# Scores and value products 512 queries wide, and eight context chunks transposed on VectorE

## The chip, the cores and the metric

The kernel runs on one core of one Trainium2 chip. The metric is the device time of one execution in microseconds; the time of a kernel is the median of its runs. TensorE is called PE below, its weight loads PEld, VectorE DVE, ScalarE ACT, GpSimd POOL, SyncE SP.

## The reference

One block of a network: cross attention of 4096 queries on 3202 context rows (8 heads of 64), a residual, then a small state-space scan of 64 states, and a row that is added to everything. All is fp32. Cut to what matters here:

```python
x = _layernorm(builder_state, g1, beta1)             # 4096 x 512 queries
base_n = _layernorm(base_state, g1, beta1)           # 3202 x 512 context rows
q, k, v = heads(q_in, Wq, bq), heads(kv_in, Wk, bk), heads(kv_in, Wv, bv)
scores = einsum('bhqd,bhkd->bhqk', q, k) * (1 / sqrt(HD))
attn = softmax(scores, axis=-1)
out = einsum('bhqk,bhkd->bhqd', attn, v)
x = residual + out.reshape(...) @ W_o.T + b_o
U = (_layernorm(x, g2, beta2) @ W_in.T + b_in) @ Bmat
s = silu(s @ A.T) + u_t                              # 4096 steps, 64 states
x = residual + states @ Cmat + mod
```

## The kernel before

**First stage, the context (to about 217 us).** The 3202 context rows are cut into 26 chunks of 128 keys (`NCH`), the last with 2 (`REST`). For each chunk c: `load_chunk` on SP, `norm_chunk` (statistics on DVE, factors on POOL, scaling on ACT), `turn_chunk` (four 128x128 transposes on PE into PSUM and one copy to `ct`, by DVE for odd chunks and by ACT for even ones), then four matmuls with `wv` for the values `pv`. After every fourth chunk (a group, `GC`) the keys `pk` of the group are made for four pairs of heads, 512 keys wide. Keys and values are stored to DRAM (`kd`, `vd`) as tiles of two chunks. Pieces of other work (weights, first queries) stand between, taken from the generator `side`.

**Second stage, attention.** The queries are cut into 8 blocks of 512 (`QB`, index Q), each block into two halves of 256 (`QU`). A unit is one half of one block for one pair of heads hp (two heads a = 0, 1 fill 128 rows); there are 64 units. A unit has 13 steps (`NDC`); a step takes two chunks of keys b = 0, 1 (the last step one chunk). A step is four pieces:
- `scores` (L713, PE): for each chunk four matmuls of 64 rows x 64 columns x 256 queries, one for each quarter of the PE array. They fill the PSUM tile `s` of 128 x 1024. A matmul in fp32 stands in the trace as two records, so eight records make one chunk.
- `weights` (L790, ACT): the exponential of `s` into an SBUF tile `p`, with the shift of the pair of heads.
- `product` (L847, PE): for each chunk four matmuls of 64x64x256 with the value tile, summed over the whole unit in the PSUM tile `po`. It has two banks, one for each half k of the keys, of which the first 256 columns are used. There is one `po` (ring `o`, one buffer).
- `add` (L798, DVE): sums `p` into `acc`, from which the denominators come.

At the second step `rest` (L784, DVE) adds the weights of the two last keys. At a unit's end: `product` first adds the last two keys (L835); `output` (ACT, L892) copies the first bank of `po`, `join` (DVE, L896) adds the second, and after that `po` is free for the next unit's first product. `fold` (DVE, L805) adds the two chunks' halves of `acc`; `swap` (ACT, L817) and `gather` (DVE, L822) add the halves of the partitions, `sums` (PE, L875) the keys, `denominators` (ACT, L914), `inverse` (DVE, L919), `scale` (DVE, L930). In the same stage the next block's queries are normalized, transposed on DVE in 32x32 squares (`flip`, L1049) and put in place by 16 small DMAs for each half block (`move`, L1061), projected (`heads`, L332), and the finished half blocks are projected (`project`: `outs` L1108, `inputs` L1165) and stored.

`load_k` and `load_v` (L379, L387) bring the tiles from DRAM on SP, 10 and 6 steps ahead; the units of the second half of a block use the tiles of the first again, apart from the last block, whose units run half by half.

**Third stage.** The scan over the states and the output rows, from about 1830 us on; it overlaps the last units.

**What sets the order.** In the second and third stage each piece is given to a planner (`Plan`): its engine, an estimated cost in ns, the pieces it comes after, a due time, and the buffers that it takes and gives back (rings, as `s`=2, `p`=18, `o`=1). `order` runs a list scheduler over these numbers and fixes the order on every engine before the program is built: an engine that comes free takes the piece with the earliest due time among those that could start. The due times are a multiple of `STEP` = 2150, and the table `SHIFT` moves the due time of each sort of piece by a number of steps. On the chip each engine then works off its list in order, and waits on semaphores.

Of the kernel before, what the change touches and what calls it, by code (L numbers as in the profile page):

```python
# [20 lines left out]
P = 128  # L21
# [12 lines left out]
FIRST = 3  # L34
WARM = 17
# [34 lines left out]
class Plan:  # L70
# [15 lines left out]
        "row.store": 11.5, "fold": 2, "rows.outs": 0.75, "heads": -12, "sample": -3, "spread": 4.75,  # L86
        "query.flip": -11, "states": -5.5, "inverse": 4.75, "extra": 10, "scale": -57.75, "rest": -1,
        "row.mod": -17, "joined0": -14.25, "b": -15, "add.l": -23, "l.stats": -34.75, "last": -4.5,
        "base": -34.75, "inverse.l": -27, "rows.inputs": 3.5, "maximum": -13.5, "fall": -19, "query.stats": -8,
        "den": 4.5, "row.scaled": 12, "l.h": -7, "row.stats": -9.25,  # L90
# [100 lines left out]
def xattn_ssm_kernel(  # L191
# [178 lines left out]
    kp = actx.enter_context(tc.tile_pool(name="kp", bufs=NDC))  # L370
    kts, vts = {}, {}

    def load_k(i, c):

        Q, hp, half = units[i]
        if half == 0 or Q == NQB - 1:
            t = kp.tile([P, 2 * CK], F32, tag="k", name=f"k_{Q}_{hp}_{half}_{c}")
            n = blocks(c) * CK
            nc.sync.dma_start(t[:, :n], kd[hp, c, :, :n])  # L379
            kts[Q, hp, c] = t  # L380

    def load_v(i, c):
        Q, hp, half = units[i]
        if half == 0 or Q == NQB - 1:
# [9 lines left out]
    steps = [(i, c) for i in range(len(units)) for c in range(NDC)]  # L394
# [150 lines left out]
    cxs, xhs, cts = {}, {}, {}  # L545
# [37 lines left out]

    with tc.manual_schedule():
# [14 lines left out]
        for c in range(4, 5):  # L599
            load_chunk(c)  # L600
# [15 lines left out]
        for c in range(NCH):  # L616
            load_chunk(c + 5)
# [4 lines left out]
            norm_chunk(c + 3)  # L622
# [17 lines left out]
            turn_chunk(c + 2)  # L640
# [19 lines left out]
            for hp in range(NC):  # L660
                pk = kps.tile([P, 512], F32, tag="k", name=f"pk_{g}_{hp}")
                for i in range(NC):
                    nc.tensor.matmul(  # L663
                        pk[:, :n_g],
                        wk[:, i, hp * P : (hp + 1) * P],
                        ct[:, i, :n_g],
                        start=(i == 0),
                        stop=(i == NC - 1),
                    )
                ks = cin.tile([P, GC * CK], F32, tag="ks", name=f"ks_{g}_{hp}")  # L670
                nc.scalar.activation(  # L671
                    ks[:, :n_g], pk[:, :n_g], AF.Identity, bias=bias[:, NC + hp : NC + hp + 1]
                )
# [31 lines left out]
    def scores(w, c):  # L705
# [3 lines left out]
        for b in range(blocks(c)):  # L709
# [69 lines left out]
    def rest(w):  # L779

        t = extras[w["at"][:2]][:, :, w["at"][2], :]
        for k in range(2):
            r, to = slice(k * HD, k * HD + REST), w["acc"][:, :, 0, k * P : (k + 1) * P]
            nc.vector.tensor_tensor(to[r], t[r], to[r], ALU.add)  # L784

    def weights(w, c):

        nb = blocks(c)
        t = w["s"][c] = sp_.tile([CK, 2, 2, QU], F32, tag="s", name=f"p_{w['name']}_{c}")
        nc.scalar.activation(t[:, :, :nb, :], w["ps"][c][:, :, :nb, :], AF.Exp, bias=w["shift"])  # L790

    def add(w, c):

        nb, t = blocks(c), w["s"][c]
# [14 lines left out]
    def halves(w, k):  # L809
        return slice(k * HD, (k + 1) * HD), w["acc"][:, :, 0, k * P : (k + 1) * P]  # L810
# [13 lines left out]
    def product(w, c):  # L824
# [6 lines left out]
        if c == NDC - 1:  # L831
            for a in range(2):
                for k in range(2):
                    r = slice(k * HD, (k + 1) * HD)
                    nc.tensor.matmul(  # L835
                        w["po"][a * HD : (a + 1) * HD, k, k * P : (k + 1) * P],
                        vx[r, hp * P + a * HD : hp * P + (a + 1) * HD],
                        extras[Q, hp][r, a, half, :],
                        start=False,
                        stop=False,  # L840
                        skip_group_check=True,
                    )
        for b in range(blocks(c)):
            for a in range(2):
                for k in range(2):
                    r = slice(k * HD, (k + 1) * HD)
                    nc.tensor.matmul(  # L847
                        w["po"][a * HD : (a + 1) * HD, k, :QU],
                        vts[Q, hp, c][r, b, a * HD : (a + 1) * HD],
                        t[r, a, b, :],  # L850
                        start=(c == 0 and b == 0),
                        stop=(c == NDC - 1),
# [3 lines left out]
    def sums(w):  # L856
# [15 lines left out]
        for a in range(2):  # L872
            for k, (k0, k1) in enumerate(((0, HD), (HD, P))):
# [4 lines left out]
                    w["acc"][k0:k1, a, 0, of],  # L878
# [9 lines left out]

    def output(w):
        Q, hp, half = w["at"]  # L890
        o = o_t[Q, hp, half] = op.tile([P, QU], F32, tag="o", name=f"o_{w['name']}", bufs=12)
        nc.scalar.copy(rows_of(w, o), rows_of(w, w["po"][:, 0, :QU], True))  # L892

    def join(w):
        o = rows_of(w, o_t[w["at"]])
        nc.vector.tensor_tensor(o, rows_of(w, w["po"][:, 1, :QU], True), o, ALU.add)  # L896

    def finish(w, i, d, plan):
# [29 lines left out]
        def scale(part):  # L928
            o = o_t[w["at"]][:, part]
            nc.vector.tensor_tensor(o, o, w["rd"][:, part], ALU.mult)  # L930

        plan.add(("output", i), "ACT", 360, partial(output, w), [("product", i, NDC - 1)], d, ["o_"])
        plan.add(("join", i), "DVE", 430, partial(join, w), [("output", i)], d + 500, [],
                 [("o", ("product", i, 0))])
        acc = [("acc", ("add", i, 1))]
        if last:
            plan.add(("sums", i), "PE", 880, partial(sums, w), [("add", i, NDC - 1)], d + 1000, ["s"], acc)
            opened = ("inverse", i, 0)
        else:
            plan.add(("fold", i), "DVE", 680, partial(fold, w), [("add", i, NDC - 1)], d + 500)  # L940
            plan.add(("swap", i), "ACT", 760, partial(swap, w), [("fold", i)], d + 600, ["rd"])
# [22 lines left out]
    def from_(d):  # L964

        return ("scores", *divmod(min(int(d / STEP), len(steps) - 1), NDC))
# [77 lines left out]

    def flip(pair, xh, t):

        nc.vector.transpose(  # L1049
            pair.rearrange("p t h -> p (t h)").rearrange("p (g t r) -> p t g r", t=2, r=TB)[:, t],  # L1050
            xh.rearrange("p (g r) -> p g r", r=TB),
        )

    def move(xn, pair, a):

        n = 2 * TB
        of = pair[a * TB : (a + 1) * TB].rearrange("p t h -> p (t h)").rearrange(
            "p (c b k) -> p b c k", b=P // TB, k=n
        )
        for b in range(P // TB):  # L1060
            nc.sync.dma_start(xn[b * TB : (b + 1) * TB, :, a * n : (a + 1) * n], of[:, b])  # L1061
# [518 lines left out]
    def unit(plan, i):  # L1580
# [3 lines left out]
        s0 = i * NDC  # L1584

        def scores_(c):
# [4 lines left out]
            w["q"] = qt[Q, hp][:, half * QU : (half + 1) * QU]  # L1591
# [20 lines left out]
        for c in range(NDC):  # L1612
            d = (s0 + c) * STEP
            g = s0 + c - NDC + AHEAD
            old = [("product", *divmod(g, NDC))] if g >= 0 else []
            part = blocks(c) / 2
            plan.add(("scores", i, c), "PE", 864 * part, partial(scores_, c), q + old, d, ["s"],
                     [("q", ("heads", Q, hp))], "quarters")
            plan.add(("weights", i, c), "ACT", 200 + 861 * part, partial(weights, w, c),
                     [("scores", i, c), ("base", first)], d + 1000, ["p"],  # L1620
                     [("s", ("scores", i, c))])
            d += LAG * STEP
            p = ("p", ("weights", i, c))
            more, gives = [], [p]
            if c == NDC - 1:
                more, gives = [("extra", first)], [p, ("extra", ("extra", first))]
            plan.add(("product", i, c), "PE", 864 if part == 1 else 650, partial(product_, c),
                     [("weights", i, c)] + ([("product", i, c - 1)] if c else []) + more,
                     d + 1000, [] if c else ["o"], gives, "quarters")
            if c:  # L1630
                before = {1: ("weights", i, 0), 2: ("rest", i)}.get(c, ("add", i, c - 1))
                plan.add(("add", i, c), "DVE", 120 + 1120 * part, partial(add, w, c),
                         [("weights", i, c), before], d + 1200,
                         ["acc"] if c == 1 else [],
                         [p] + ([("p", ("weights", i, 0))] if c == 1 else []))
            if c == 1:
                plan.add(("rest", i), "DVE", 860, partial(rest, w), [("add", i, 1), ("extra", first)],
                         d + 1300, [], [("extra", ("extra", first))])
        d += 2000
        finish(w, i, d - 40 * STEP if w["last"] else d, plan)  # L1640
# [241 lines left out]
    with tc.manual_schedule():  # L1882
# [5 lines left out]
                xn=1, xh=2, max=2, rd=2, o_=12,  # L1888
# [5 lines left out]
        for i, (Q, hp, half) in enumerate(units):  # L1894
            d = unit(plan, i)
            if (hp, half) == (1, 0) and Q + 1 < NQB:
                queries(plan, Q + 1, i * NDC * STEP)
# [97 lines left out]
```

## Time and profile before

| what | value |
|---|---|
| median of 3 runs | 1946.28 us (1945.93 to 1947.35) |
| the profiled execution's own time | 1949.57 us |
| its span, first to last instruction | 1947.8 us |
| granted TensorE clock | 0.997 |
| busy PE, PEld, DVE, ACT, POOL | 1927.4, 1259.5, 1465.8, 1169.8, 216.5 us |

A busy time is the time in which at least one instruction of a group was in flight. PE matmuls overlap: a record lasts longer than the time until the next one starts, and four quarters of the array work at once. So a PE time is read here from the starts of records, not from their lengths. The timeline view has one row for a run of equal instructions: its start, its length, and the number of records. The view by stretches gives the busy time of each engine in a stretch. The view of groups gives line, engine, operation, tiles, shapes, and then busy time, mean length of one in ns, idle time before them and what ended it.

### The profile page before, as it was taken

How to read it: one execution, taken by the hardware profiler on the slowest of the kernel's cores; microseconds unless marked ns; L12 is line 12 of the kernel's file. 1: busy time of each engine (PE TensorE's matmuls, PEld its weight loads, DVE VectorE, ACT ScalarE, POOL GpSimd, SP SyncE). 2: the span in 40 equal slices, each digit the busy share in tenths (PEclk: the TensorE clock that was granted, in tenths of full speed). 3: DMA queues.
4: the chain of work that ended last, by engine and by line, in shares of the span. 5: the costliest groups of instructions: out<-in, count | busy, mean ns of one | idle time of the engine just before them, and what ended most of it. 6: DMA issues, size and time to landing. Idle time of an engine off the chain costs nothing.

```text
span 1947.8 us, 66909 instructions
## 1 busy us (share of the span) xinstructions
PE 1927.4 (99%) x29088; PEld 1259.5 (65%) x29088; DVE 1465.8 (75%) x1982; ACT 1169.8 (60%) x1630; POOL 216.5 (11%) x370
## 2 busy tenths in 40 slices
PE   9999999999999999999999999999999999999997
PEld 5444577676666666666667666766666666766675
DVE  5311389688877887888868887888788887978776
ACT  2233477576666566667657665666666766756643
POOL 2111000001200120001100120012001110011105
PEclk9999999999999999999999999999999999999998
DMA  5533233123432243233412342224322331544576
GB/s 190 177 100 108 66 88 107 55 87 90 124 87 81 82 121 77 72 91 80 127 49 87 92 124 79 81 86 118 86 72 82 99 107 60 152 130 136 168 192 207
DMA packets 251541, 205.32 MB, mean 105 GB/s; under 512 B 85416, under 2 KB 224680, under 8 KB 251244
## 3 DMA queue, kind: packets, MB, share of 16 engines
q1 hardware_dynamic: 247224, 194.37, 34.9%
q10 hardware_dynamic: 4020, 6.62, 1.1%
q8 instruction: 231, 3.78, 0.8%
q14 instruction: 66, 0.54, 0.1%
HBM read 156.32 MB, written 29.88 MB: 96 GB/s over the span
## 4 chain that ended last, share of the span: by engine, by line


## 5 line engine op out<-in xcount | busy, mean ns | idle before, releaser
L790 ACT ACTIVATE p<-s,shifts 128x1024 f32<-128x1024 f32 (+1 forms) x832 | 891.8, 1081 | 479.7 <-PE s L713 465.1
L798 DVE TENSOR_TENSOR acc<-p,acc 128x1024 f32<-128x1024 f32 (+1 forms) x704 | 829.7, 1179 | 136.8 <-ACT p L790 100.8
L713 PE MATMUL s<-q,k 64*64 64x256 f32 x12800 | 833.6, 377 | 0.2 <-ACT p L790 0.2
L847 PE MATMUL po<-p,v 64*64 64x256 f32 x12800 | 832.6, 377 | 0.0
L713 PEld LDWEIGHTS s<-q,k 64*64 64x64 f32 x12800 | 488.6, 133 | 208.1 <-ACT p L790 15.0
L847 PEld LDWEIGHTS po<-p,v 64*64 64x64 f32 x12800 | 485.0, 133 | 193.4 <-issue 16.9
L919 DVE RECIPROCAL rd<-rd 128x256 f32<-128x256 f32 (+1 forms) x64 | 110.1, 1722 | 70.8 <-ACT rd L914 70.8
L1102 POOL TENSOR_TENSOR xr<-xr,rowb 128x512 f32<-128x512 f32 x30 | 40.9, 1370 | 996.6 <-DMA k<-kd 527.8
L332 PE MATMUL pq<-xn,wq 128*128 128x512 f32 x248 | 110.7, 598 | 0.0
L1108 PE MATMUL pa<-wo,o 128*128 128x512 f32 x240 | 107.0, 599 | 0.0
L630 PE MATMUL pv<-wv,ct 128*128 128x512 f32 (+1 forms) x208 | 92.7, 596 | 1.4 <-DVE wv L413 0.9
L663 PE MATMUL pk<-ct,wk 128*128 128x512 f32 (+1 forms) x224 | 88.9, 550 | 0.0
L798 DVE TENSOR_TENSOR acc<-p,p 128x1024 f32<-128x1024 f32 x64 | 80.3, 1255 | 10.3 <-ACT p L790 10.0
L582 DVE COPY ct<-tp_c 128x512 f32<-128x512 f32 (+1 forms) x13 | 8.4, 649 | 105.7 <-PE tp_c L303 105.7
L332 PEld LDWEIGHTS pq<-xn,wq 128*128 128x128 f32 x248 | 45.8, 190 | 55.3 <-issue 55.3
L1108 PEld LDWEIGHTS pa<-wo,o 128*128 128x128 f32 x240 | 44.4, 190 | 56.0 <-issue 56.0
L663 PEld LDWEIGHTS pk<-ct,wk 128*128 128x128 f32 x224 | 39.2, 190 | 42.6 <-issue 42.6
L630 PEld LDWEIGHTS pv<-wv,ct 128*128 128x128 f32 (+1 forms) x208 | 36.9, 186 | 44.1 <-issue 41.3
L341 ACT ACTIVATE q<-pq,bias 128x512 f32<-128x512 f32 x31 | 21.3, 688 | 73.4 <-PE pq L332 73.4
L671 ACT ACTIVATE ks<-pk,bias 128x512 f32<-128x512 f32 (+1 forms) x28 | 18.0, 642 | 74.7 <-PE pk L663 72.4
L822 DVE TENSOR_TENSOR acc<-swap,acc 64x256 f32<-64x256 f32 x126 | 55.3, 439 | 8.9 <-ACT swap L817 7.2
L784 DVE TENSOR_TENSOR acc<-x,acc 2x256 f32<-2x256 f32 x128 | 53.0, 414 | 2.6
(219 smaller groups left out, 1210.4 us busy)
## 6 DMA issues: line engine op xcount, KB each, us to landing
k<-kd SPq DMA_DIRECT2D x432, 128.0 KB, 2.3
v<-vd SPq DMA_DIRECT2D x432, 128.0 KB, 2.2
xn<-x SPq DMA_DIRECT2D x448, 32.0 KB, 1.9
xr<-in_x_dram SPq DMA_DIRECT2D x30, 256.0 KB, 3.3
x1d<-xr SPq DMA_DIRECT2D x30, 256.0 KB, 2.2
x<-in_x_dram SPq DMA_DIRECT2D x28, 256.0 KB, 3.5
cx<-in_ctx_dram SPq DMA_DIRECT2D x25, 256.0 KB, 3.3
vd<-vs SPq DMA_DIRECT2D x25, 256.0 KB, 2.4
```

What stands on the lines that cost most here:

```text
L332: nc.tensor.matmul(pq, wq[:, i, hp * P : (hp + 1) * P], xn[:, i, :], start=(i == 0), stop=(i == NC - 1),)
L630: nc.tensor.matmul(pv[h * HD : h * HD + n, :H], ct[:, k, o : o + n], wv[:, k, :], start=(i == 0), stop=(i == NC // parts - 1), skip_group_ ...
L663: nc.tensor.matmul(pk[:, :n_g], wk[:, i, hp * P : (hp + 1) * P], ct[:, i, :n_g], start=(i == 0), stop=(i == NC - 1),)
L713: nc.tensor.matmul(s[k0 : k0 + HD, a, b, :], kts[(*w["at"][:2], c)][r, b * CK + k0 : b * CK + k0 + HD], q[r], start=True, stop=True, skip_ ...
L784: nc.vector.tensor_tensor(to[r], t[r], to[r], ALU.add)
L790: nc.scalar.activation(t[:, :, :nb, :], w["ps"][c][:, :, :nb, :], AF.Exp, bias=w["shift"])
L798: nc.vector.tensor_tensor(w["acc"][:, :, :nb, :], t[:, :, :nb, :], before[:, :, :nb, :], ALU.add)
L822: nc.vector.tensor_tensor(of[r], w["swap"][r], of[r], ALU.add)
L847: nc.tensor.matmul(w["po"][a * HD : (a + 1) * HD, k, :QU], vts[Q, hp, c][r, b, a * HD : (a + 1) * HD], t[r, a, b, :], start=(c == 0 and b ...
L919: nc.vector.reciprocal(w["rd"][:, part], (w["pd"] if last else w["rd"])[:, part])
L1102: nc.gpsimd.tensor_tensor(v["x"], v["x"], rowb, ALU.add)
L1108: nc.tensor.matmul(v["pa"], o_t[Q, c, half][:, t * P : (t + 1) * P], wo[:, c, :], start=(c == 0), stop=(c == NC - 1),)
```

## The change

1. For the first seven query blocks (`wide(Q)`: all but the last), the two halves of a block become one unit. A step takes one chunk of keys and all 512 queries: four matmuls of 64x64x512 in place of eight of 64x64x256. A unit has 25 steps in place of 13 + 13. `s`, `p`, `acc` keep their sizes; `po` is used in full.
2. The two halves of `acc` are now the two halves of the queries, so wide units have no `fold`. `rest` and the product with the last two keys take both halves of the queries at once.
3. At a wide unit's end both halves must leave `po`: two `output` copies on ACT and two new copies `aside` on DVE; `join` then adds two SBUF tiles, later, and no longer frees `po`.
4. In the first stage the chunks 8, 9, 12, 13, 16, 17, 20, 21 (`flips`) are no longer transposed on PE: `flip_pair` transposes two chunks on DVE in squares of 32, `move_pair` puts them in place with 16 DMAs on SP. The keys of such a pair come to stand in another order, the same for keys and values. Chunks are loaded 6 ahead in place of 5.
5. The rings of key and value tiles have 12 buffers in place of 13; a wide unit loads a tile at every second step.
6. A new table `SHIFT`, and changed costs for some pieces.

```diff
+FLIPS = 2
@@ class Plan
-        "row.store": 11.5, "fold": 2, "rows.outs": 0.75, "heads": -12, "sample": -3, "spread": 4.75,
...
+        "row.store": 22, "fold": 22.75, "rows.outs": 1.25, "heads": -15.25, "sample": -4.25, "spread": 2.75,
...
+        "den": -18.5, "row.scaled": 20, "l.h": -44, "row.stats": -8.5, "row.load": 1.25, "aside": -10,
+        "join": -2.25, "query.move0": -12.25, "scale.l": 11.25, "swap": -2, "output": -4.5,
@@
-    kp = actx.enter_context(tc.tile_pool(name="kp", bufs=NDC))
+    kp = actx.enter_context(tc.tile_pool(name="kp", bufs=NDC - 1))
+    def wide(Q):
+        return Q < NQB - 1
+    def loads_at(i, c):
+        Q, hp, half = units[i]
+        if not wide(Q):
+            return Q, hp, half, c
+        c, odd = divmod(half * NDC + c, 2)
+        return Q, hp, half, None if odd else c
@@ first stage
+    def flips(c):
+        return FLIPS <= c // GC < NCH // GC and c % GC < 2
+    def flip_pair(c):
+        g = c // GC
+        pairs[g] = wp.tile([P, NC, H], F32, tag="raw_" + "vqkq"[g - FLIPS], name=f"pair_{g}")
+        for t in range(2):
+            flip(pairs[g][:, :2], xhs.pop(c + t), t)
+    def move_pair(c, *parts):
+        g = c // GC
+        if 0 in parts:
+            cts[g] = ctp.tile([P, NC, GC * CK], F32, tag="ct", name=f"ct_{g}")
+        for a in parts:
+            move(cts[g][:, :, : 2 * CK], pairs[g][:, :2], a)
...
-            norm_chunk(c + 3)
+            if not flips(c + 3):
+                norm_chunk(c + 3)
+            elif c % GC == 1:
+                norm_chunk(c + 3)
+                norm_chunk(c + 4)
+            if flips(c + 1) and c % GC == GC - 1:
+                move_pair(c + 1, 0, 1)
...
-            turn_chunk(c + 2)
+            if not flips(c + 2):
+                turn_chunk(c + 2)
+            elif c % GC == 2:
+                flip_pair(c + 2)
...
+                if hp < 2 and flips(c + 1):
+                    move_pair(c + 1, 2 + hp)
@@ scores
+        if w["wide"]:
+            c0, b = divmod(c, 2)
+            for k0 in (0, HD):
+                for a in range(2):
+                    r = slice(a * HD, (a + 1) * HD)
+                    nc.tensor.matmul(
+                        s[k0 : k0 + HD, a].rearrange("p h j -> p (h j)"),
+                        kts[(*w["at"][:2], c0)][r, b * CK + k0 : b * CK + k0 + HD],
+                        q[r],
...
@@ product
-                        w["po"][a * HD : (a + 1) * HD, k, :QU],
-                        vts[Q, hp, c][r, b, a * HD : (a + 1) * HD],
-                        t[r, a, b, :],
+                        w["po"][a * HD : (a + 1) * HD, k, : 2 * QU if w["wide"] else QU],
+                        (vts[Q, hp, c // 2][r, c % 2] if w["wide"] else vts[Q, hp, c][r, b])[
+                            :, a * HD : (a + 1) * HD
+                        ],
+                        t[r, a].rearrange("p h j -> p (h j)") if w["wide"] else t[r, a, b, :],
@@ a unit's end
+    def aside(w):
+        w["aside"] = op.tile([P, QU], F32, tag="aside", name=f"aside_{w['name']}", bufs=2)
+        nc.vector.tensor_copy(rows_of(w, w["aside"]), rows_of(w, columns(w, 1), True))
     def join(w):
+        if "aside" in w:
+            o = o_t[w["at"]]
+            nc.vector.tensor_tensor(o, o, w["aside"], ALU.add)
+            return
...
+        if aside_:
+            plan.add(("aside", i), "DVE", 430, partial(aside, w), ended, d, ["aside"], o)
...
+            if not w["of"]["wide"]:
+                plan.add(("fold", i), "DVE", 680, partial(fold, w), [folded], d + 500)
@@ unit
-            g = s0 + c - NDC + AHEAD
+            g = s0 + c - NDC + 1 + AHEAD
-            plan.add(("product", i, c), "PE", 864 if part == 1 else 650, partial(product_, c),
+            plan.add(("product", *at), "PE", (864 if part == 1 else 432) + 108 * (c == w["end"]), partial(product_, c),
```

More of the change, by code (lines that the diff above doesn't have):

```diff
@@ L393, in xattn_ssm_kernel @@
     units += [(NQB - 1, hp, half) for half in range(2) for hp in range(NC)]
-    steps = [(i, c) for i in range(len(units)) for c in range(NDC)]
+    steps = [
+        (i, c) for i, (Q, hp, half) in enumerate(units) for c in range(NDC if half == 0 or not wide(Q) else NDC - 1)
+    ]
+    place = {at_: g for g, at_ in enumerate(steps)}
     AHEAD_K, AHEAD, REF = 10, 6, 7
@@ L1590, in scores_ @@
                     load(*steps[g + ahead])
-            w["q"] = qt[Q, hp][:, half * QU : (half + 1) * QU]
+            w["q"] = qt[Q, hp][:, half * QU : (half + 1) * QU] if not wide(Q) else qt[Q, hp]
             scores(w, c)
```

166 lines of the change are left out of this document (95 added, 71 removed).

## The prediction

> **What bounds the kernel now.** I read the page's busy times first, then the busy time by stretches, then PE's waits inside the attention stage, then the starts of PE records in the timeline.
>
> ```profile
> span 1947.8 us, 66909 instructions
> PE 1927.4 (99%) x29088; PEld 1259.5 (65%) x29088; DVE 1465.8 (75%) x1982; ACT 1169.8 (60%) x1630; POOL 216.5 (11%) x370
> ```
> ```profile
> 100.00:200.00 100.00, 100.00 (x282) 47.36 (x281) 15.82 (x37) 32.79 (x52) 15.72 (x45) 1.00 0.36 105
> 1000.00:1200.00 200.00, 200.00 (x3304) 133.09 (x3300) 163.47 (x209) 129.09 (x173) 21.18 (x32) 1.00 0.32 89
> ```
> ```profile
> PE pu L1165 <- DMA k<-kd: 1.4, 1, 1.4
> PE sm L733 <- ACT ks L671: 0.2, 1, 0.2
> ```
>
> PE is busy in all of both stretches (after the bounds and the length of the stretch: PE, PEld, DVE, ACT, POOL, granted clock, DMA share, GB/s). The last fence is the whole list of PE's waits between 200 and 1830 us: 1.6 us. So PE sets the end through the first two stages; DVE has 200 - 163.5 = 36.5 us free of each 200. But busy does not mean that PE works at its best pace, so the question is what PE does in that time:
>
> ```profile
> L713 PE MATMUL s<-q,k 64*64 64x256 f32 x12800 | 833.6, 377 | 0.2 <-ACT p L790 0.2
> L332 PE MATMUL pq<-xn,wq 128*128 128x512 f32 x248 | 110.7, 598 | 0.0
> L1274 PE MATMUL z<-u,a_t 64*64 64x512 f32 x12 | 3.6, 589 | 0.0
> ```
> ```profile
> 1029.07 1.04 PE L713 MATMUL s<-q,k 64*64 64x256 f32 x16
> ...
> 1037.70 1.04 PE L713 MATMUL s<-q,k 64*64 64x256 f32 x16
> 1038.57 0.29 PE L755 MATMUL sm<-twice,m 64*64 64x64 f32 x8
> ```
> ```profile
> 100.75 7.03 PE L663 MATMUL pk<-ct,wk 128*128 128x512 f32 x16
> 107.62 3.60 PE L630 MATMUL pv<-wv,ct 128*128 128x512 f32 x8
> ...
> 111.05 0.60 PE L303 MATMUL tp_c<-ident,xh_c 128*128 128x128 f32 x4
> 111.49 0.60 PE L303 MATMUL tp_x<-ident,xh_x 128*128 128x128 f32 x4
> ```
>
> From 1029.07 to 1038.57 run 11 rows of 16 records, score and product in turn: 9.50 / 11 = 0.8636 us for 16, or 215.9 ns for four records, one in each quarter of the array. The row of 16 full records of 512 columns takes 107.62 - 100.75 = 6.87 us, 429.4 ns for each. Twice 215.9 is 431.8. So four quarters of 256 columns already run at nearly the pace per column of a full record; 2.4 ns is what is left to gain for each 512 columns.
>
> **The wide units (-6.7 us).** Seven of eight blocks turn wide. Scores and products have 2 x 12800 records; 7/8 of them are 22400, and they become 11200 records 512 wide, 2800 groups of four. If a group takes 429.4 ns, the gain is 2800 x 2.4 = 6.7 us. No 512-wide group in four quarters is in the trace; the nearest are the 64x512 records of the scan, whose mean length of 589 against 377 ns grows by 212 ns, as much as 256 columns cost above. Bounds: 0 (the overhead goes with columns) to 431.8 - (215.9 + 212) = 3.9 ns and 10.9 us (a wide group is longer by those 212 ns alone). I take 6.7, the row of the same width. Weight loads halve, but PEld is busy 133 of 200 us beside PE and no PE wait hangs on it: nothing. The last keys' product has the same columns as before: nothing.
>
> **The transposes (-3.5 us).** The row of four `tp_c` records lasts 111.49 - 111.05 = 0.44 us until the next start. Eight chunks without it: 8 x 0.44 = 3.5 us, in a stage in which PE has no gap.
>
> ```profile
> L303 PE MATMUL tp_c<-ident,xh_c 128*128 128x128 f32 x100 | 15.2, 274 | 0.4 <-ACT xh_c L287 0.4
> ```
>
> The record itself is 274 ns long. [...] The starts, 0.11 us apart, say that they overlap, so the sum has 3.5.
>
> What takes their place has cover only if it comes in time. DVE makes eight flips of 0.69 us, in a stage where it is busy 16 of 100 us. SP issues 4 x 16 more small DMAs:
>
> ```profile
> L1061 SPq DMA_DIRECT2D xn<-x x448: 585/599/2001, 281.3 to 1796.2; - x150
> DMA to landing us min/median/max: 1.9/1.9/4.6
> ```
>
> So four DMAs take 2.4 us to issue and 1.9 to land. In the order of SP, two moves (8 DMAs) stand before the value store of a group's last chunk, the third behind the key stores of hp 0, the fourth behind those of hp 1. Counted from that chunk's first value matmul, hp 1's keys are through PE after 3.43 + 2 x 3.43 = 10.3 us; with the ACT copy and two stores the fourth move starts at about 12.2 and lands at 16.5. The next chunk's values start after 3.43 + 4 x 3.43 = 17.2, and need the first two moves; the one behind it, 3.4 us later, needs the rest. It fits by 0.7 us at least. Bounds: 0 to 4 groups x 2.5 us late = 10; I take 0. Queued behind a late move on SP would be the value store and the next chunk loads, six chunks ahead.
>
> **Changes of PE between quarters and full array (-2.1 us).**
>
> ```profile
> 999.80 1.48 PE L713 MATMUL s<-q,k 64*64 64x256 f32 x24
> 1001.21 3.70 PE L332 MATMUL pq<-xn,wq 128*128 128x512 f32 x8
> 1004.84 1.96 PE L847 MATMUL po<-p,v 64*64 64x256 f32 x32
> ```
>
> 24 records in quarters take 6 x 215.9 = 1.30, so full records could start at 1001.10; they start 0.11 later. Eight of them take 3.44, and the quarters start again 0.19 later than that: 0.30 us for a trip. In the built order of PE the attention and the last stage have 44 such trips before and 37 after: the fourth `heads` of each of blocks 1 to 7 now stands right behind the third. 7 x 0.30 = 2.1 us. The price is four `heads` in a row, 13.7 us without scores; 18 buffers of `p` and the two of `s` cover it, as they covered three in a row.
>
> **DVE and ACT.**
>
> ```profile
> L798 DVE TENSOR_TENSOR acc<-p,acc 128x1024 f32<-128x1024 f32 x640 | 785.6, 1227 | 131.5 <-ACT p L790 98.9 <-DVE acc L798 1.4
> L798 DVE TENSOR_TENSOR acc<-p,acc 128x512 f32<-128x512 f32 x64 | 44.1, 689 | 5.3 <-ACT p L790 1.9
> L805 DVE TENSOR_TENSOR acc<-acc 128x512 f32<-128x512 f32 x63 | 44.2, 701 | 1.4
> L784 DVE TENSOR_TENSOR acc<-x,acc 2x256 f32<-2x256 f32 x128 | 53.0, 414 | 2.6
> L896 DVE TENSOR_TENSOR o<-po,o 128x256 f32<-128x256 f32 x64 | 27.0, 422 | 15.0 <-ACT o L892 14.5
> L930 DVE TENSOR_TENSOR o<-o,rd 128x256 f32<-128x256 f32 x62 | 29.1, 470 | 1.4
> L790 ACT ACTIVATE p<-s,shifts 128x1024 f32<-128x1024 f32 x768 | 847.6, 1113 | 476.8 <-PE s L713 462.4 <-PE sm L755 4.9
> L790 ACT ACTIVATE p<-s,shifts 128x512 f32<-128x512 f32 x64 | 44.3, 692 | 2.9 <-PE s L713 2.6
> ```
>
> For each wide unit: 24 full adds (29.4 us) in place of 22 full and 2 half ones (28.4): +1.1. No folds: -1.4. `rest` twice at the 512-wide 0.69 in place of four times 0.41: -0.3. Two `aside` at 0.42: +0.8. `join` from SBUF at the 0.47 of `scale`: +0.1. Together +0.3 us on DVE in about 51 (1630 us for 32 pairs of units); on ACT 25 x 1.113 in place of 24 x 1.113 + 2 x 0.692: -0.3. Both stay behind PE: nothing on the path.
>
> **A unit's end (+1.3 us).** With one `po`, the next unit's first product waits until `po` is empty. Before:
>
> ```profile
> 1047.32 0.61 PE L847 MATMUL po<-p,v 64*64 64x256 f32 x8
> 1047.75 1.91 PE L713 MATMUL s<-q,k 64*64 64x256 f32 x32
> ```
> ```profile
> 1047.78 1.23 DVE L798 TENSOR_TENSOR acc<-p,p 128x1024 f32<-128x1024 f32 x1
> 1049.04 0.84 DVE L784 TENSOR_TENSOR acc<-x,acc 2x256 f32<-2x256 f32 x2
> 1049.91 0.42 DVE L896 TENSOR_TENSOR o<-po,o 128x256 f32<-128x256 f32 x1
> ```
>
> Here DVE first finished an add and `rest`, and `join` ended 2.58 us after the last product; PE had scores and a sample to do meanwhile. After the change there are 28 such ends in place of 56. The order puts two scores between most of them, 2 x 0.86 = 1.73 us of cover, and `aside` twice is 0.84; so DVE may be late by 0.9 us less a semaphore's 0.2. Directly ahead of `aside` stands `rest` (1.38) at 14 ends, a `gather` or an add at the others. If `rest` has just begun when the product ends, PE stands 1.38 - 0.7 = 0.7 us; if it is through, 0. Bounds 0 to 28 x 0.7 = 20 us; below nothing is excluded, since no wait of these is in PE's list now. I take 1.3, near the lower end: `aside` has an early due time, so DVE takes nothing else once it can start, and a quarter of the ends at 0.2 us is what that leaves.
>
> **Sum.** -6.7 - 3.5 - 2.1 + 1.3 = -11.0 us. The profiled execution has a span of 1947.8 and 1949.57 us in all, 1.8 us around it; it would be 1938.6. The median of the runs is 3.3 below that execution: 1946.3 - 11.0 = 1935.3, say 1935. The new due times act through the order alone, counted above; the third stage's order on PE is nearly the old one: within 2 us either way.
>
> **Rivals.**
> - *The overhead goes with the columns*: the 2.4 ns are not for each record. Against it: 429.4 at 512 and 215.9 at 256 are not in proportion. It leaves 1935 + 6.7 = 1942.
> - *A unit's end stalls PE* (the other side). Place: the first product of a wide unit, behind `aside` on DVE. From 12.3 / 28 = 0.44 us at each end on, the change is slower than before; at the 0.7 above the time is 1946.3 - 12.3 + 20 = 1954. For it: DVE is busy 82% in this stage and `rest` has doubled. Against: before, with the same single `po`, twice as many ends and DVE as busy, PE had no wait there.
> - *The moves are late*: 4 groups x 2.5 us: 1945.
> - *The quarters are bound by overheads, as busy times suggest*: 833.6 us for 12800 records is 260 ns for four, against 446 (110.7 / 248) for a full one of 512; that would be 75 ns for each of 2800 groups, 209 us: 1736. Against: the starts; each row's tail of 0.18 us is counted twice, in L713 and in L847.
>
> [...]
>
> **How the numbers follow.** About 0.2% (3.9 us) is what a measurement can tell from no change: the bounds are 1942.4 and 1950.2. My forecast, 1929 to 1942: 0.70. Overhead with columns: 0.08, half of it within 0.2%. Unit ends: 0.11, most of it slower, some within. Moves late: 0.08, mostly within. Busy times: 0.01. The rest, 0.02, is slower for reasons of order that I do not see. Faster 0.70 + 0.04 + 0.02 + 0.01 = 0.77; within 0.04 + 0.03 + 0.06 = 0.13 and rounding, 0.14; slower 0.09. The range, 1928 to 1948, takes in the late moves and the first part of the stalling ends, and leaves about 0.12 out.
>
> **What would show it.** Starts of rows of eight wide records 0.858 to 0.859 us apart (0.864: the first rival). No `tp_c` for eight chunks, and no PE wait on `ct` by a DMA between 60 and 190 us (if there is one: the third). PE's list of waits between 200 and 1830 us with under 3 us on `po` or `aside`; over 12 us makes the prediction wrong. DVE near 165 of 200 us in the attention stage. A gain of 30 us or more would show that starts are not what PE is bound by.

## The result and the profile after

| what | before | after |
|---|---|---|
| median | 1947.05 us (6 runs, 1945.93 to 1950.39) | 1978.07 us (6 runs, 1972.2 to 1981.52) |
| span of the profiled execution | 1947.8 us | 1976.8 us |
| granted clock | 0.997 | 0.991 |

The change makes the kernel slower: ratio 1.0154, 95% interval 1.0137 to 1.017, about 31 us. The forecast was 1935, so 43 us are to be found: the gains that did not come, or the losses that were not seen.

The busy times on the page of after:

```profile
PE 1928.7 (98%) x17632; PEld 895.1 (45%) x17632; DVE 1477.8 (75%) x1930; ACT 1166.1 (59%) x1598; POOL 226.6 (11%) x370
```

PE is as busy as before (1928.7 against 1927.4 us) in a span that is 29 us longer. So PE now stands. A stretch of after that was full before (bounds and length; PE, PEld, DVE, ACT, POOL; granted clock, DMA share, GB/s), and its list of PE's waits between 200 and 1860 us (total, times, longest):

```profile
1000.00:1200.00 200.00, 196.08 (x1826) 81.89 (x1819) 172.91 (x210) 133.82 (x177) 20.75 (x32) 1.00 0.31 84
```
```profile
PE pq L334 <- DMA xn<-x: 16.0, 6, 3.8
PE po L931 <- PE s L779: 7.8, 17, 1.0
PE pu L1251 <- DMA xn<-x: 4.2, 1, 4.2
PE po L931 <- issue: 3.4, 2, 1.9
...
```

The list of before had 1.6 us in all. This one has 31.6: 20.2 in which `heads` (L334) and once `inputs` (L1251) wait for their `move`, and 11.2 at the first product of a unit (L931). Two more numbers belong to it. The group of the `heads`:

```profile
L334 PE MATMUL pq<-xn,wq 128*128 128x512 f32 x248 | 118.2, 637 | 16.0 <-DMA xn<-x 16.0
```

Before, the same 248 records took 110.7 us at 598 ns: 7.5 us more without a wait, which the clock has to explain. (Counted from starts, the slow records alone come to 9.7 us; the busy times also hold the tail of each row, and before has more rows.) And the list leaves small gaps out: counted from the starts of all PE records, gaps of over 0.16 us ahead of a unit's first product come to 16.4 us in 24 places. Set against the same 28 ends of wide units in `e1` below, where hardly one stalls, the first products come 15.4 us later in all, at 20 of the ends. The three losses are 20.2 + 7.5 + 16.4 = 44 us; less the 12.3 us of gains that the prediction's sum had, 32 stay.

**The moves.** SP's queue in after, ahead of the `heads` of a block:

```profile
529.96 2.52 SPq L579 DMA_DIRECT2D xn<-x  x4
532.53 0.59 SPq L394 DMA_DIRECT2D k<-kd  x1
533.16 0.43 SPq L402 DMA_DIRECT2D v<-vd  x1
...
552.59 3.25 SPq L579 DMA_DIRECT2D xn<-x  x4
```

And the same place in before:

```profile
536.63 12.19 SPq L1061 DMA_DIRECT2D xn<-x  x16
548.92 2.43 SPq L379 DMA_DIRECT2D k<-kd  x5
```

Before, 16 moves stood in one row and the loads of keys and values waited behind them, five in a row. In after a key and a value load stand behind these four moves, and so it goes on, mostly; the last move's issue ends 552.59 + 3.25 - (536.63 + 12.19) = 7.0 us later. The number of loads is the same in both kernels; this row of the list of DMA issues stands on both pages, and the values' row has 432 too:

```profile
k<-kd SPq DMA_DIRECT2D x432, 128.0 KB, 2.3
```

On PE, after first, then before:

```profile
552.97 1.09 PE L1251 MATMUL pu<-xn,wc 128*64 128x128 f32 x16
557.62 15.56 PE L334 MATMUL pq<-xn,wq 128*128 128x512 f32 x32 [3.56 <-DMA xn<-x]
573.11 1.09 PE L779 MATMUL s<-q,k 64*64 64x512 f32 x8
```
```profile
551.16 10.57 PE L332 MATMUL pq<-xn,wq 128*128 128x512 f32 x24
561.65 1.09 PE L847 MATMUL po<-p,v 64*64 64x256 f32 x16
```

The `heads` of after wait 3.56 us. Then their 32 records take 573.11 - 557.62 = 15.49 us, where 32 x 0.4294 would be 13.74: another 1.75. The two stretches of after behind the wait say why:

```profile
558.00:562.00 4.00, 4.00 (x7) 1.63 (x7) 1.12 (x3) 0.00 (x0) 0.00 (x0) 0.65 0.83 237
562.00:566.00 4.00, 4.00 (x11) 1.76 (x10) 0.00 (x0) 0.69 (x1) 0.00 (x0) 1.00 0.80 235
```

The granted clock is 0.65 in the first 4 us, with 7 records, and 1.00 in the next, with 11. So this wait of 3.56 us cost 5.3. The rows at this document's end show two shorter ones.

**A unit's end.** All engines' timeline of after, one end of a unit (DVE, ACT and PE rows):

```profile
518.13 1.90 PE L779 MATMUL s<-q,k 64*64 64x512 f32 x16
518.37 0.37 ACT L981 COPY o<-po 128x256 f32<-128x256 f32 x1 [0.18 <-PE po L931]
...
519.53 0.42 DVE L985 COPY aside<-po 128x256 f32<-128x256 f32 x1
519.99 0.37 ACT L981 COPY o<-po 128x256 f32<-128x256 f32 x1 [1.25 <-DVE aside L985]
...
520.39 0.43 DVE L985 COPY aside<-po 128x256 f32<-128x256 f32 x1 [0.44 <-ACT o L981]
...
520.92 1.95 PE L931 MATMUL po<-p,v 64*64 64x512 f32 x16 [0.90 <-PE s L779]
```

ACT and DVE do not empty `po` side by side. ACT copies, DVE copies, ACT has waited 1.25 us for DVE, DVE waits 0.44 for ACT: four copies in turn. `output` reads only the first bank and `aside` only the second, but both name the one tile `po`, and the waits go by the tile: in `e1` below, with a tile for each bank, ACT and DVE start 0.04 us apart. PE's note names a matmul as releaser, since that ended last; the product starts 0.1 us after the last `aside`. At this end a second thing adds to it: DVE was at two `gather` (L905) until 519.50, and ACT's second copy stood behind DVE's first. Counted from starts over the ends of wide units, the usual chain of four copies is through 2.35 to 2.4 us after the last product's start, and the two scores cover 2.13: about 0.35 us each, some 8 us of the 16.4. At nine ends DVE came late as well, as here, and they make up the rest.

Two announced signs came true, so the gains are there. Rows of eight wide records of after:

```profile
544.99 1.07 PE L931 MATMUL po<-p,v 64*64 64x512 f32 x8
...
549.28 1.07 PE L779 MATMUL s<-q,k 64*64 64x512 f32 x8
```

Five rows lie between these starts: 4.29 / 5 = 0.858 us. And the first score sample, which ends the first stage, in after and in before:

```profile
212.84 0.64 PE L811 MATMUL sm<-q,kx 64*64 64x256 f32 x2
```
```profile
216.55 0.64 PE L733 MATMUL sm<-q,kx 64*64 64x256 f32 x2
```

3.7 us earlier, with 3.5 forecast.

### The profile page after: what moved, and what is told of

The parts are those of the page before. It is cut to its first block, busy times and chain, and to the rows that moved or that the text cites. A ratio compares the mean times of both kernels' runs of the same rounds, so it can differ in the third digit from the quotient of the medians.

```text
span 1976.8 us, 43992 instructions
## 1 busy us (share of the span) xinstructions
PE 1928.7 (98%) x17632; PEld 895.1 (45%) x17632; DVE 1477.8 (75%) x1930; ACT 1166.1 (59%) x1598; POOL 226.6 (11%) x370
## 4 chain that ended last, share of the span: by engine, by line
## 5 line engine op out<-in xcount | busy, mean ns | idle before, releaser
L873 ACT ACTIVATE p<-s,shifts 128x1024 f32<-128x1024 f32 x804 | 884.5, 1109 | 416.9 <-PE s L779 352.9
L881 DVE TENSOR_TENSOR acc<-p,acc 128x1024 f32<-128x1024 f32 (+1 forms) x732 | 900.3, 1230 | 188.1 <-ACT p L873 141.3
L931 PE MATMUL po<-p,v 64*64 64x512 f32 (+1 forms) x7200 | 845.5, 543 | 11.6 <-PE s L779 7.8
L779 PE MATMUL s<-q,k 64*64 64x512 f32 x5600 | 735.5, 590 | 0.0
L931 PEld LDWEIGHTS po<-p,v 64*64 64x64 f32 x7200 | 303.4, 133 | 359.5 <-issue 310.2
L779 PEld LDWEIGHTS s<-q,k 64*64 64x64 f32 x5600 | 238.2, 133 | 332.2 <-issue 293.6
L1188 POOL TENSOR_TENSOR xr<-xr,rowb 128x512 f32<-128x512 f32 x30 | 50.3, 1681 | 903.9 <-DMA xr<-in_x_dram 782.9
L334 PE MATMUL pq<-xn,wq 128*128 128x512 f32 x248 | 118.2, 637 | 16.0 <-DMA xn<-x 16.0
L791 PE MATMUL s<-q,k 64*64 64x256 f32 x1600 | 110.3, 380 | 0.0
L334 PEld LDWEIGHTS pq<-xn,wq 128*128 128x128 f32 x248 | 49.8, 204 | 78.7 <-issue 74.3
L905 DVE TENSOR_TENSOR acc<-swap,acc 64x256 f32<-64x256 f32 x126 | 54.6, 433 | 35.0 <-ACT swap L900 33.1
L900 ACT COPY swap<-acc 64x256 f32<-64x256 f32 x126 | 50.8, 403 | 48.2 <-DVE o L1027 27.2
L791 PEld LDWEIGHTS s<-q,k 64*64 64x64 f32 x1600 | 68.8, 134 | 21.2 <-issue 3.8
L881 DVE TENSOR_TENSOR acc<-p,p 128x1024 f32<-128x1024 f32 x36 | 45.1, 1254 | 27.3 <-ACT p L873 26.9
```

Source lines behind the costliest of these rows:

```text
L334: nc.tensor.matmul(pq, wq[:, i, hp * P : (hp + 1) * P], xn[:, i, :], start=(i == 0), stop=(i == NC - 1),)
L779: nc.tensor.matmul(s[k0 : k0 + HD, a].rearrange("p h j -> p (h j)"), kts[(*w["at"][:2], c0)][r, b * CK + k0 : b * CK + k0 + HD], q[r], sta ...
L791: nc.tensor.matmul(s[k0 : k0 + HD, a, b, :], kts[(*w["at"][:2], c)][r, b * CK + k0 : b * CK + k0 + HD], q[r], start=True, stop=True, skip_ ...
L881: nc.vector.tensor_tensor(w["acc"][:, :, :nb, :], t[:, :, :nb, :], before[:, :, :nb, :], ALU.add)
L900: nc.scalar.copy(w["swap"][r], of[(1 - k) * HD : (2 - k) * HD])
L905: nc.vector.tensor_tensor(of[r], w["swap"][r], of[r], ALU.add)
```

## The experiments

Each ratio is to the kernel before, run beside it on the same chip, with its 95% interval; the median of before was 1946.51 for the first four, 1945.64 for `e5`, `e7`, `e8`, and 1946.41 for `e9`, `e10`. The theory: after loses on two things, the crowd on SP and the copies in turn. The rivals: DVE comes late to `aside` because it is full; the new due times have spoilt the order.

| run | kernel | median, us | ratio |
|---|---|---|---|
| `e1_two_po` | after, `po` as two tiles | 1947.51 | 1.0008 (0.9996 to 1.0019) |
| `e2_loads_on_act` | after, loads issued by ACT | 2052.84 | 1.0542 (1.0526 to 1.0558) |
| `e3_both` | `e1` and `e2` together | 2029.35 | 1.043 (1.0415 to 1.0444) |
| `e4_flips_alone` | before, with the transposes on DVE | 1939.56 | 0.9963 (0.995 to 0.9977) |
| `e5_moves_planned_longer` | `e1`, moves planned at 3600 ns | 1937.26 | 0.9958 (0.9944 to 0.9972) |
| `e7_old_due_times` | `e1`, due times of before | 1967.08 | 1.0106 (1.0089 to 1.0123) |
| `e8_paired_loads` | `e1`, loads of two tiles each | 1927.26 | 0.9907 (0.989 to 0.9923) |
| `e9_paired_loads_one_po` | after, loads of two tiles each | 1940.77 | 0.9968 (0.9956 to 0.998) |
| `e10_without_flips` | `e8`, all transposes on PE | 1931.63 | 0.9934 (0.9916 to 0.9951) |

Where the time of the profiled executions goes, in us, by the starts of PE records: to the first score sample, from there to the last product of block 6 (the seven wide blocks), from there to the last product of all (the last block), and the rest. The profiled execution of before is about 3 us slower than its medians.

| run | first stage | blocks 0 to 6 | last block | rest |
|---|---|---|---|---|
| before | 216.6 | 1461.1 | 212.2 | 57.9 |
| after | 212.8 | 1489.6 | 217.3 | 57.1 |
| `e1_two_po` | 212.7 | 1466.0 | 213.4 | 56.1 |
| `e4_flips_alone` | 213.2 | 1461.2 | 209.2 | 54.0 |
| `e5_moves_planned_longer` | 212.7 | 1450.1 | 212.4 | 59.6 |
| `e7_old_due_times` | 212.6 | 1483.4 | 210.3 | 58.3 |
| `e8_paired_loads` | 212.7 | 1449.0 | 208.9 | 54.0 |
| `e9_paired_loads_one_po` | 212.7 | 1461.5 | 209.6 | 55.9 |
| `e10_without_flips` | 215.7 | 1449.4 | 209.0 | 56.0 |

### `po` as two tiles

```diff
-            w["po"] = ps_o.tile([P, 2, 2 * QU], F32, tag="o", name=f"po_{w['name']}")
+            w["po"] = [ps_o.tile([P, 2 * QU], F32, tag=f"o{k}", name=f"po{k}_{w['name']}") for k in range(2)]
...
-                        w["po"][a * HD : (a + 1) * HD, k, : 2 * QU if w["wide"] else QU],
+                        w["po"][k][a * HD : (a + 1) * HD, : 2 * QU if w["wide"] else QU],
```

The same two banks, but a name for each; the first block's `heads` and the last stage, which use the banks too, take one tile each as well.

> The changed kernel, with po as two tiles of one PSUM bank each (bank k of the keys), so that the ACT copies (output) and the DVE copies (aside) of a unit's end touch different tiles. Order and due times are the same. Theory 'chained copies': in the changed kernel output and aside wait for each other in turn (0.37 + 0.42 + 0.37 + 0.42 us), which is longer than the 1.73 us of cover; apart, PE's waits ahead of first products fall from 16 us to under 5, and the time from 1978 to 1963 to 1968 us. Rival 'DVE is late': rest and the adds ahead of aside on DVE are what PE waits for; then the waits stay over 11 us and the time at 1973 or more.

The timeline of all engines of this run, at the same end of a unit (PE, ACT and DVE rows):

```profile
516.84 1.90 PE L779 MATMUL s<-q,k 64*64 64x512 f32 x16
517.07 0.65 ACT L981 COPY o<-po 128x256 f32<-128x256 f32 x2 [0.15 <-PE po L931]
517.11 0.76 DVE L985 COPY aside<-po 128x256 f32<-128x256 f32 x2 [0.86 <-PE po L931]
...
518.55 1.47 PE L931 MATMUL po<-p,v 64*64 64x512 f32 x12
```

Both engines copy at once and are through at 517.87, 0.7 us before the product is due; the product starts without a wait. The waits of PE that are left (between 200 and 1830 us):

```profile
PE pq L334 <- DMA xn<-x: 12.5, 6, 2.5
PE pu L1251 <- DVE acc L881: 2.6, 1, 2.6
PE po L931 <- DVE aside L985: 0.3, 1, 0.3
```

The stall at the product went from 11.2 us in the list to 0.3, with the work of DVE and the due times as they were. By starts, the copies are through 1.44 to 1.74 us after the last product in nearly all wide units, also where `rest` holds DVE until 0.83 us after that start: 0.4 us are to spare. In `e8` below, with the same two tiles, `rest` holds DVE until 1.45 us at one end, and the next product still starts on time: DVE's lateness does not show. So the turns are what the stall hangs on, and a late DVE adds to it only where they have used up the cover. The median fell by 30.6 us, more than these: the waits on moves fell from 20.2 to 12.5 with them (the wait of `inputs`, 4.2 before, is now 2.6 and ends with DVE), and records at a low clock from 9.7 to 4.9 us (records spaced more than usual within the `heads`, counted from starts). The longest wait of the `heads` is now 2.5 us in place of 3.8. Why the moves are less late when units end sooner was not tested.

### The loads taken off SP

```diff
-            nc.sync.dma_start(t[:, :n], kd[hp, c, :, :n])
+            (nc.scalar if Q and wide(Q) else nc.sync).dma_start(t[:, :n], kd[hp, c, :, :n])
```

The same for the values. `e3` has this edit and the one above.

> The changed kernel, with the key and value loads of the wide units (blocks 1 to 6) issued from ACT's queue in place of SP's. Theory 'SP is crowded': the moves of the next block's queries now share SP with a load every 0.86 us of PE work, land 3 to 4 us late, and heads wait; then PE's waits ahead of heads (17.6 us), the slow records behind them (9.7) and most of the 4.4 us ahead of inputs go, and the time is 1948 to 1956 us. Rival 'the flips are late or the due times too early': SP's loads do not matter, heads still wait 12 us or more, and the time is over 1968.

> Both edits together. If the two theories hold and do not hide each other: 1978 - 30 - 12 = 1936 us, 1933 to 1942, faster than before. If another cause stands behind them (wide records slower, due times): 1950 or more.

Both missed, by about 100 and 90 us. The waits of PE on moves for the `heads` are gone, but PE waits for ACT. The costliest wait in `e2` between 200 and 1900 us on PE, then one row of ACT's list, then SP's, ACT's and PE's timelines at one place:

```profile
PE s L779 <- ACT p L873: 59.8, 35, 3.2
```
```profile
ACT p L873 <- DMA k<-kd: 47.4, 73, 2.1
```
```profile
927.85 11.15 SPq L579 DMA_DIRECT2D xn<-x  x16
```
```profile
931.08 0.33 ACTq L394 DMA_DIRECT2D k<-kd  x1
...
932.74 1.52 ACT L1092 ACTIVATE xh_x<-x,nm_x,rstd_x 128x512 f32<-128x512 f32 x2 [3.65 <-DMA k<-kd]
934.17 2.09 ACT L873 ACTIVATE p<-s,shifts 128x1024 f32<-128x1024 f32 x2
```
```profile
935.31 3.51 PE L779 MATMUL s<-q,k 64*64 64x512 f32 x16 [2.30 <-ACT p L873]
```

The issue of a load is short, 0.33 us for keys in the median, and 0.44 for a value load at 603.70. But ACT works off its list in order. Here a key load stands at its head and is issued only at 931.08; ACT does nothing for 3.65 us, and the exponentials behind, and PE's next scores, come late. Counted from starts, 55 of the 59.8 us follow a place like this one, where ACT stood idle in front of a key load. What such a load waits for, no row names. At 36 of the 42 places at which ACT stood idle for over 1 us in front of a load (between 400 and 1750 us), SP was issuing DMAs for 89% or more of the idle time, as in the row above; over the whole stretch it does so for 20%. Whether the two queues hold each other up, or the loads wait for a buffer, no run takes apart. The runs show that the waits of the `heads` hang on SP's queue, but say nothing of what the time would be without them: the cure cost more than the complaint.

### The first stage alone

The change's edits of the first stage (`flips`, `flip_pair`, `move_pair`, loads 6 ahead) on the kernel before; units, due times and the rest as before.

```diff
+FLIPS = 2
...
-        for c in range(4, 5):
+        for c in range(4, 6):
...
-            turn_chunk(c + 2)
+            if not flips(c + 2):
+                turn_chunk(c + 2)
+            elif c % GC == 2:
+                flip_pair(c + 2)
```

> The kernel before, with the first stage's part of the change alone (eight chunks transposed on DVE). As the first score of the changed kernel starts 3.7 us earlier than before, the theory says 1943.5 us, 1942 to 1945. Rival: the first stage's gain is lost later, because the attention stage's order was fitted to the old start: 1946 to 1949.

7.0 us faster (4.5 to 9.7 by the interval), twice what was expected. The first score sample came 3.4 us earlier (213.18 against 216.55), as forecast. By the table the wide blocks' share is as long as before, and the last block and the rest are 3.1 and 4.0 us shorter; up to 3 us of this can be the slow profiled execution of before. `e10` gives the other side: without these edits, the best kernel below loses 4.4 us. So the first stage is worth 3.4 by its own stage, 4.4 and 7.0 in two whole kernels; where the rest of the 7.0 comes from is open.

### Fewer, larger loads

```diff
-    kp = actx.enter_context(tc.tile_pool(name="kp", bufs=NDC - 1))
+    kp = actx.enter_context(tc.tile_pool(name="kp", bufs=NDC // 2))
...
-        if c is not None:
-            t = kp.tile([P, 2 * CK], F32, tag="k", name=f"k_{Q}_{hp}_{half}_{c}")
+        if c is not None and c % 2 == 0:
+            t = kp.tile([P, 2, 2 * CK], F32, tag="k", name=f"k_{Q}_{hp}_{half}_{c}")
...
-            nc.sync.dma_start(t[:, :n], kd[hp, c, :, :n])
+            nc.sync.dma_start(t[:, :m, :n], kd[hp, c : c + m, :, :n].rearrange("t p n -> p t n"))
```

The same for the values: two tiles with one DMA, so that SP issues half as many. Keys are loaded 8 steps ahead in place of 10, values 3 in place of 6, so they also stand at other places in SP's list; the runs do not separate this from their number. `e8` has it on top of `e1`, `e9` on after alone, so the four kernels after, `e1`, `e9`, `e8` have each loss in and out.

> The changed kernel with two po tiles (as e1, 1947.5 us), and one DMA for two key tiles, and one for two value tiles, so that SP issues 7 + 7 loads for a unit in place of 13 + 13; the order on PE, DVE and ACT is that of e1. Theory 'SP is crowded by the loads': the moves come 3 us earlier, the waits ahead of heads (14.0 us in e1) and the slow records behind them (4.9) go, and the time is 1927 to 1934 us. Rival 'flips or due times': heads wait as before, over 10 us, and the time is 1943 or more.

> The changed kernel with the paired loads alone, po as one tile. If the two causes add, the waits ahead of heads go and those ahead of first products (16.4 us in the changed kernel) stay over 10 us: 1943 to 1958 us. If the copies at a unit's end only waited because SP was late, they go too: under 1933.

`e8` is the fastest of all, 1927.26 us, 18.4 below the kernel before. The first row of its list of PE waits (200 to 1830 us; it has two more of 0.2), a stretch, and SP's queue:

```profile
PE pq L334 <- issue: 0.2, 1, 0.2
```
```profile
1000.00:1200.00 200.00, 200.00 (x1784) 76.44 (x1780) 167.24 (x202) 130.51 (x175) 20.90 (x32) 1.00 0.32 92
```
```profile
545.68 0.54 SPq L394 DMA_DIRECT2D k<-kd  x1
...
546.78 2.53 SPq L581 DMA_DIRECT2D xn<-x  x4
```

The last move is issued at 549.3, against 555.8 in after. In `e9` the list of waits reads (200 to 1860 us):

```profile
PE po L933 <- PE s L781: 4.6, 12, 1.0
...
PE pq L334 <- DMA xn<-x: 0.3, 1, 0.3
```

The wait on moves went from 20.2 to 0.3 us, those at a unit's end stayed; their gaps come to 12.8 us in 29 places, counted from starts (11.0 against the same ends of `e8`), and 1940.77 - 1927.26 = 13.5 us is what `e8` gains on it. From after, the two cures give 30.6 and 37.3 us alone but 50.8 together: 17 us hang on both, and the time of `e9` was a little under the range expected. A late unit end and a late move make each other worse; how was not taken apart.

### The moves planned longer

```diff
-                plan.add((*ks[0], f"move{a}"), "SP", 2600, partial(move_, a),
+                plan.add((*ks[0], f"move{a}"), "SP", 3600, partial(move_, a),
```

On top of `e1`: the planner's cost for four moves, nothing on the chip is made longer.

> As e1, with the planner's cost of a move (four DMAs) at 3600 ns in place of 2600, so that it knows of the loads between them; the order changes everywhere. Theory: heads are put later, waits ahead of heads under 3 us, 1927 to 1935 us. Rival 'the new due times alone put heads too early': the planner still does, waits over 10 us, 1943 or more.

10 us faster than `e1`, and 2 us over the range expected. No wait of the `heads` on a move is left in its list. By the table its wide blocks take 1450.1 us, nearly the 1449.0 of `e8`; what it loses to `e8` comes behind them, 3.5 us in the last block and 5.6 in the rest, where the edit has changed the order too. So in the wide blocks the lateness can be cured in the order as well, without a change of the loads.

### The due times of before

On top of `e1`: the table `SHIFT` as it was.

> As e1, with the table SHIFT of the kernel before. If the new due times are what hurts, this is faster than e1 by 10 us or more (under 1938 us). If they are a fit to the wide units that only misses SP's loads, the old ones are no better: 1945 to 1975 us, with PE's waits ahead of first products and heads together over 15 us.

20 us slower than `e1`, and within the range expected for due times that fit no better; the waits on moves are longer than the 12.5 us of `e1`. One row of its list of PE waits:

```profile
PE pq L333 <- DMA xn<-x: 16.4, 6, 3.7
```

So going back to the old due times does not cure the loss; for wide units they are worse.

### Without the first-stage part

`e8` with `FLIPS = 9`, so that no chunk is transposed on DVE.

> e8 (1927.3 us) with all context chunks transposed on PE again. By the term of the prediction, 3.5 us more: 1929.5 to 1932.5 us. If the gain of 7 us seen for the flips alone is theirs: 1934.

4.4 us slower than `e8`, as expected; the first score sample is 2.96 us later (215.65 against 212.69).

## Why the prediction was wrong

- **What bounds the kernel** was right for before, but it was carried over: that PE waits for next to nothing is a property of the order on SP as well.
- **The wide units (-6.7)**: the pace was right, 0.858 us for eight records where 0.859 was announced. The first rival (overhead goes with the columns, 0.864) falls.
- **The transposes (-3.5)**: right by the first score sample, 3.7 us earlier. `move_pair` came in time: no PE wait on `ct` is in the list of after between 60 and 200 us, so the third rival falls.
- **Changes of PE (-2.1)**: the fourth `heads` stood behind the third, as said (32 records in a row). The cover of 13.7 us of `heads` by `p` was enough in `e8`, where no wait stands behind them. The price of a trip was not measured again.
- **DVE and ACT (nothing)**: right. `e8` shows PE at 200 of 200 us with DVE at 167.24, where 165 was announced.
- **A unit's end (+1.3)**: a step that failed, in size and in its mechanism. Measured: about 16 us in after, 0.3 to 0.4 us at eleven ends and 0.7 to 2.0 at nine. The rival on the other side had 0.7 for an end that stalls, 20 us in all; that this came near is luck, for it put DVE's `rest` in front of `aside`. Of the nine late ends `rest` stood there at three and a `gather` at six, and `e1` has the same `rest` and no stall. The prediction counted "`aside` twice is 0.84", as if ACT worked beside it; in turn the four copies are 0.37 + 0.42 + 0.37 + 0.43 = 1.59 us and the handovers. The 0.2 us set aside for a semaphore was the author's estimate; in after the product above starts 0.1 us after the last `aside`. The copies use up the cover at every end that has two scores and no sample between (0.35 us over), and only then does a busy DVE add to it. The old kernel had one copy on each engine at an end, so its trace could not show a second turn; the two readers of one tile in the code could.
- **"The new due times act through the order alone, counted above"**: the step that failed altogether. The change's item 5, a load at every second step, was listed and never priced. The number of loads is the same, so it looked free. But before, all loads of a block and pair of heads came in the unit of the first half, and the unit of the second left SP to the moves; now each unit carries its loads to its end, between the moves. The order on PE was compared and the order on SP was not. Price: 20.2 us of waits and 7.5 us of low clock, though some of it hangs on the late unit ends as well (`e1`).
- **The sum.** -11.0 was forecast. With both losses out, the kernel that has all the gains is 18.4 us faster than before, so the gaining side was too small. By the table, `e8` against before: 3.9 us in the first stage, where 3.5 stood; 12.0 in the wide blocks, where 6.7 + 2.1 stood and the pace of 0.858 alone gives 2800 x (431.8 - 429.0) = 7.8; and 7.2 behind them, where nothing stood, of which some 3 are the slow profiled execution of before. What shortens the last block and the rest is open. With both losses in, +31.
- **The chances.** No rival reached 1978: the crowd on SP had only its part of "the rest, 0.02", an order that the prediction did not see. Unit ends had 0.11 for 1954; they alone, with SP cured, are `e9`: 1940.8, under the 1946. So even that rival would have left the change faster. Nor do the late moves alone make it slower: they are `e1`, level with before. It took both to make it slower.

## What to carry to other kernels

When a change spreads the same number of DMAs over more of a unit, look at what else stands in that queue, and who waits for the last of it: compare the built order on SP as closely as that on PE. Where two engines empty a PSUM tile, try one tile for each reader: from the one tile of after the four copies went in turn, 1.59 us in all, and from the two tiles of `e1` ACT and DVE started 0.04 us apart. A wait of PE of 1.85 us cost nearly twice its length in after: in the 4 us behind it the granted clock was 0.57 (below), and 0.43 x 4 = 1.7 us is lost with it.

## What the runs showed of the hardware

In after the clock also fell behind shorter waits than that of 3.56 us, though not behind all of them. PE's timeline, and the stretches behind two of the waits:

```profile
985.67 1.53 PE L334 MATMUL pq<-xn,wq 128*128 128x512 f32 x3 [2.48 <-DMA xn<-x]
...
1198.86 2.66 PE L334 MATMUL pq<-xn,wq 128*128 128x512 f32 x3 [1.85 <-DMA xn<-x]
```
```profile
986.00:990.00 4.00, 4.00 (x10) 1.71 (x9) 2.61 (x4) 0.62 (x1) 0.00 (x0) 1.00 0.85 255
1199.00:1203.00 4.00, 4.00 (x6) 1.65 (x7) 3.07 (x4) 0.00 (x0) 0.00 (x0) 0.57 0.89 252
1203.00:1207.00 4.00, 4.00 (x10) 1.71 (x9) 0.00 (x0) 0.69 (x1) 0.00 (x0) 1.00 0.84 246
```

The wait of 2.48 us left the clock at 1.00, and behind that of 1.85 us it was 0.57 over 4 us, then 1.00 again. Of the six waits of `heads` in after, 1.85 to 3.78 us long, a lower clock followed five, 0.50 to 0.66 over 4 us, all but that of 2.48. So in this trace the length of a wait alone does not tell what it costs; what else decides was not shown.

- A DMA issue on ACT's queue in `e2` took 0.33 us for keys in the median, and for values 0.44 at 603.70 and 1.40 at 607.14, and the exponentials behind it waited until it was out: 64 us of ACT's waits in `e2` name the loads (47.4 for keys, 16.8 for values), and the kernel lost 75 us. Most of the loss came where the load itself was held back, while SP was issuing.
- A load of 256 KB was issued in about as much time as one of 128 KB: 0.41 to 0.59 us in `e8` (SP's rows from 522 to 553 us), against 0.32 to 0.59 and once 1.69 in after (525 to 558 us; 0.38 in the median of all). Half as many loads took SP about half the time, an estimate from these rows.
- In `e1` ACT from 517.07 and DVE from 517.11 read a bank of `po` each, 0.65 and 0.76 us long, side by side. The turns in after, from 518.37 to 520.82, came from the tile's name, not from the banks.
